# First-layer products with x as two 64-row halves beside each other, pairs two to four

## The chip, the cores and the metric

The kernel runs on one core of a Trainium2 chip. The core has a matrix engine (TensorE, PE in the profile, its weight loads PEld), a vector engine (VectorE, DVE), a scalar engine with function tables (ScalarE, ACT), GpSimd (POOL) and a queue engine that issues most transfers (SyncE, SP). The engines run at the same time, each its own instructions in order, and wait for each other on semaphores. TensorE writes into eight banks of PSUM, each of 128 partitions by 512 numbers of 32 bits; DVE and ACT read them from there. The metric is the time of one execution on the device, in microseconds, as the median of several runs.

## The reference

There are 8 batches of 512 tokens of width 256, and for each batch 64 context rows. The reference computes, per batch:

```python
nx = layer_norm(x, ln_gamma, ln_beta)
q, k, v = nx @ Wq, ctx @ Wk, ctx @ Wv            # v: 64 rows
weights = softmax(q @ k.T / sqrt(256))           # tokens x 64
evidence = weights @ v
combined = concat(nx, evidence, cond)            # width 768
p = softmax(combined @ router_W + router_b)      # 3 experts
h[e] = silu(combined @ e_w1[e] + e_b1[e])        # width 512 for each expert
routed = sum over e of p[e] * (h[e] @ e_w2[e] + e_b2[e])
g = sigmoid(silu(combined @ gate_w1 + gate_b1) @ gate_w2 + gate_b2)
out = x + g * (routed @ out_w + out_b)
```

All of it is in 32-bit floating point. The change touches the part of `h[e]` and of the gate's first layer that comes from `nx` and from `evidence`.

## The kernel before, in words

**Pairs.** The eight batches are worked as four pairs j = 0 to 3. The two batches of a pair, i = 0 and i = 1, share products: a 2 x 2 block of a weight matrix (two halves of the 256 inputs by two chunks of 128 outputs) times a 2 x 2 block of x (two halves of the inputs by two batches) is computed with seven products instead of eight, by sums and differences of the blocks (Winograd's form of Strassen's scheme). The sums over weights are `ws`, those over x are `T` (`combine_x`, L640). `nx_product` (L843) issues one of the seven for a group n of two output chunks: numbers 1, 4, 6 and 7 go into the accumulator `U[n]`, 2 into `Y[n]`, 3 and 5 into `Z[n]`. Group 0 is the gate's first layer (`S["hg"]`), groups 1 to 6 are the experts' 12 chunks, two groups to an expert (`PAIRS`). A product contracts 128 rows: it is one matrix instruction of 128x128 weights by 128x512 data, issued by `product` (L794 to L796).

**Evidence products.** The evidence part needs only 64 rows, since a batch has 64 context rows. The context's values are multiplied with the first layer's weights once per pair (`value_weights`, L771 the products, L778 the copy, L785 a difference), which gives `vw` with batch i in rows 64i to 64i + 63. The softmax weights `wT` lie likewise. `evidence` (L803) issues products of 64 rows, two beside each other: one for batch 0 on rows 0 to 63 and one for batch 1 on rows 64 to 127, into different banks. Each group needs four: into `U`, `Y` and twice into `Z`. In the gate the fourth goes into a bank `W` of its own.

**What is read between the products.** The seven-product form reads an accumulator while it grows. `keep_part` (L838, ACT) copies a state of `U` or `Z` into the chunk of h of one batch, `add` (L835, DVE) adds another accumulator's state to it, `silu` (L829, ACT) applies the function, from h or, for the last, straight from PSUM. `weigh` (L880 and L876, DVE) multiplies h with the router's probabilities `pb` and forms a difference for the second layer.

**Order.** Everything is ordered by hand. For each pair `gate_layer` (L883) comes first and ends with a group of eight evidence products; then `expert_layer` (L927) three times, each ending with eight (the last with four); then `outputs` (L1008), the gate's second layer and the experts' second layers in runs of six or more products. So the first layers hold four groups of evidence products per pair, and full products between them. Steps for the next pair are hung on points of this order by `put` (L1268): `statistics` (L547, L548), `deviation` (L551, ACT, which loads the Sqrt table and afterwards the Silu table), `normalize` (L556, L559), `store_x` (L616, to DRAM on SP's queue), `regroup_x` and `load_x_blocks` (L475, SP's queue), `router_part` (L600), `gate_differences` (L1005), and for the pair itself `router`, `spread_probabilities` (L748 the transposed `prT`; L751 and L755 `pd` and `pb` on POOL's queue) and `value_weights` of expert 2 in expert 1's point "B" (L771). Points of `outputs` are "begin", "gate", "P1", "P5", "P6" and so on.

**Banks.** Each accumulator has a bank by number (`bank`); a new one in the same bank waits until the readers of the former are through. Smaller products take a bank from a list that `spares` sets and `misc` rotates.

Of the kernel before, what the change touches and what calls it, by code (L numbers as in the profile page):

```python
# [8 lines left out]
F32 = mybir.dt.float32  # L9
AF = mybir.ActivationFunctionType  # L10
ALU = mybir.AluOpType
# [5 lines left out]
def kernel(  # L17
# [77 lines left out]

    spare = []

    def bank(i, name):
        return psum.tile([P, 512], F32, tag=f"b{i}", name=name)

    def spares(*banks):
        spare[:] = banks
# [447 lines left out]
    def deviation(j, i):  # L550
        nc.scalar.activation(S["sd", j][:, i, :], S["mv", j][:, i, :, 1], AF.Sqrt, bias=eps_t)  # L551

    def normalize(b):
        mv, sd = (S[n, b // 2][:, b % 2] for n in ("mv", "sd"))
        rstd = work.tile([P, NT], F32, tag="rstd", name=f"rstd_{b}")
        nc.vector.reciprocal(rstd, sd)  # L556
        xn = x_sb[b]
        for t in range(NT):
            nc.vector.tensor_scalar(  # L559
                xn[:, t, :], x_sb[b][:, t, :], mv[:, t, 0:1], rstd[:, t : t + 1], ALU.subtract, ALU.mult  # L560
            )
        S["xn", b] = xn
# [25 lines left out]
            nc.gpsimd.memset(S["lg", j][:, 0, :], 0.0)  # L588
        return S["lg", j]

    def router_part(b):

        j, a = b // 2, b % 2
        lg = logits(j)
        junk = work.tile([P, H], F32, tag="pv", name=f"junk_{b}", bufs=1)
        sums = lg[:, 2, a * NT : (a + 1) * NT]
        if j == 0:
            sums = work.tile([P, NT], F32, tag="ls", name=f"ls_{b}")
        for t in range(NT):
            nc.vector.scalar_tensor_tensor(  # L600
                junk, S["xn", b][:, t, :], 1.0, gg, ALU.mult, ALU.mult, accum_out=sums[:, t : t + 1]
            )
        if j == 0:

            for h in range(2):
                for q in range(NT):
                    nc.gpsimd.tensor_copy(
                        lg[side(a, h), 2, q::NT], sums[q * TB : (q + 1) * TB, 2 * h : 2 * h + 2]
                    )
# [149 lines left out]
    def by_side(flat):  # L759
        return flat.rearrange("p (h t) -> p h t", h=2)  # L760
# [30 lines left out]
    Z_BANKS = ((5, 7), (0, 2), (5, 7))  # L791
    U, Z, Y = {}, {}, {}

    def product(ps, lhsT, rhs, start=False):  # L794

        nc.tensor.matmul(ps, lhsT, rhs, start=start, stop=True, skip_group_check=not start)  # L796

    def fresh(j, e):

# [40 lines left out]
    def hidden(j, q, k, i):  # L840
        return S["h", i, 2 * q // RC][:, (2 * q + k) % RC, :]

    def nx_product(j, n, which, start=False):  # L843
        q = GROUPS[n]
        c = 2 * q
        A, Bx, T_ = S["nxT", 2 * j], S["nxT", 2 * j + 1], S["T", j]

        def a(k, d):
            return w1[:, k, (c + d) * P : (c + d + 1) * P]

        dst, lhsT, rhs = {
            1: (U, a(0, 0), A[:, 0, :]),
            2: (Y, a(1, 0), A[:, 1, :]),
            3: (Z, ws[:, S4, q, :], Bx[:, 1, :]),
            4: (U, a(1, 1), T_[:, 2, :]),
            5: (Z, ws[:, S1, q, :], T_[:, 0, :]),
            6: (U, ws[:, S2, q, :], T_[:, 1, :]),
            7: (U, a(0, 1), Bx[:, 0, :]),
        }[which]
        product(dst[n], lhsT, rhs, start=start)  # L860

    late = []

# [6 lines left out]

    def weigh(j, most):
        for m, i, d in late[:most]:
            q = GROUPS[m]
            if d is None:
                b12 = hidden(j, q, 0, 1)
                nc.vector.tensor_tensor(b12, b12, hidden(j, q, 0, 0), ALU.subtract)  # L876
            else:
                h = hidden(j, q, d, i)
                h = by_side(h)
                nc.vector.tensor_tensor(h, h, S["pb", j][:, i, :, 2 * q // RC, :], ALU.mult)  # L880
        del late[:most]

    def gate_layer(j, steps):  # L883
        n = 0
        for i in range(2):
            for k in range(KH):
                S["hg", i, k] = hpool.tile([P, T], F32, tag=f"hg{i}{k}", name=f"hg_{2 * j + i}_{k}")
        U[n], Z[n], Y[n] = (bank(i, f"ps_{u}_{j}_{n}") for i, u in ((0, "u"), (2, "z"), (3, "y")))
        nx_product(j, n, 1, True)
        keep_part(n, 0, 0, U[n])  # L890
        if j == 0:
            anchor_columns(E)
            anchor_columns(0)
        spares(7, 5)
        nx_product(j, n, 5, True)
        keep_part(n, 1, 1, Z[n])
        nx_product(j, n, 2, True)
        nx_product(j, n, 6)
        keep_part(n, 1, 0, U[n])
        nx_product(j, n, 3)  # L900
        for step in steps.get("gate", ()):
            step()
        nx_product(j, n, 7)
        add(n, 1, 1, U[n])
        for step in steps.get("gate end", ()):
            step()
        W = bank(1, f"ps_w_{j}")
        fresh(j, 0)
        evidence(j, [(m, True) for m in PAIRS[0]], W=W)

        add(n, 0, 0, Y[n])
        add(n, 1, 0, Z[n])
        add(n, 1, 1, W)
        silu(j, n, 0, 0)
# [12 lines left out]
    def expert_layer(j, e, steps):  # L927
# [65 lines left out]
        else:  # L993
            evidence(j, [(m, False) for m in (a, b)])

    gate_sums = {}

    def gate_differences(j):
        (b11, b12), (b21, b22) = [[S["hg", i, k] for i in range(2)] for k in range(2)]
        t2, t3, t4 = (  # L1000
            work.tile([P, T], F32, tag=tag, name=f"g_{name}_{j}", bufs=n)
            for name, tag, n in (("t2", "r21", 1), ("t3", "yb", 2), ("t4", "yb", 2))
        )
        for dst, p, m in ((b12, b12, b11), (t2, b22, b12), (t3, t2, b11), (t4, b21, t2)):
            nc.vector.tensor_tensor(dst, p, m, ALU.subtract)  # L1005
        gate_sums[j] = t2, t3, t4

    def outputs(j, steps):  # L1008
        last = j == NP - 1
# [21 lines left out]
        u, z, y = (bank(i, f"ps_g{n}_{j}") for n, i in (("u", 0), ("z", 2), ("y", 4)))  # L1031
        product(u, gw[0][0], b11, start=True)
        product(z, gw2s[:, S1, :], b12, start=True)
        finish_groups(j, PAIRS[-1])
        nc.scalar.copy(g1, u)
        nc.scalar.copy(g22, z)
        spares(6, 7, 4)
        product(y, gw[0][1], b21, start=True)
        product(u, gw2s[:, S2, :], t2)
        nc.scalar.copy(g2, u)  # L1040
        finish_odd(j, PAIRS[-1])
        gate(0, 0, g1, y)
        product(z, gw2s[:, S4, :], b22)
        gate(0, 1, g2, z)
        product(u, gw[1][0], t3)
        gate(1, 1, g22, u)
        run("begin")
        weigh(j, 99)
        run("gate")

        NQ = NE // 2
# [148 lines left out]
    with tc.manual_schedule(engines=None):  # L1200
# [62 lines left out]
        for j in range(NP):  # L1263
# [38 lines left out]
                put(within, (1, "D"), combine_second, 2)  # L1302
            if j:
                put(within, "gate", value_weights, j, 1, nc.scalar.copy, False)
                put(within, (0, "S"), value_differences, j, 1)
                put(within, (0, "S"), router, j)
                put(within, (0, "S"), spread_probabilities, j)
            if j and j + 1 < NP:
                put(within, (0, "B"), statistics, 2 * j + 3, 0, NT)
            put(within, (0, "C" if j == 0 else "B"), value_weights, j, 2)  # L1310
            put(within, (1, "C"), load_x_blocks, 2 * j)
            put(within, (2, "A"), gate_differences, j)
            put(within, (2, "C"), load_x_blocks, 2 * j + 1)
            if j + 1 < NP:
                b0, b1 = 2 * j + 2, 2 * j + 3
                if j + 2 < NP:
                    put(between, "begin", load_x, b0 + 2)
                    put(between, "begin", load_x, b1 + 2)
                put(within, (0, "A" if j else "D"), statistics, b0, 0, NT)
                if j == 0:  # L1320
                    put(within, (0, "D"), statistics, b1, 0, NT)
                for i in range(2):
                    put(within, (0, "D") if j else (1, "S"), deviation, j + 1, i)
                for b in (b0, b1):
                    put(within, (1, "W" if j else "S"), normalize, b)
                    put(within, (1, "W" if j else "S"), store_x, b)
                put(within, (1, "C"), regroup_x, b0)
                put(within, (1, "A" if j else "B"), router_part, b0)
                put(within, (1, "D" if j else "B"), router_part, b1)
                put(between, "begin", transpose_blocks, b0)  # L1330
                put(between, "gate", regroup_x, b1)
                put(between, "begin", value_weights, j + 1, E)
                put(between, "begin", store_router_rows, j + 1)
                put(between, "begin", spread_router_rows, j + 1)
                put(between, "P5", transpose_blocks, b1)
                put(between, "P2", scores, j + 1)
                put(between, "P2", combine_x, j + 1, nc.gpsimd)
                put(between, "P7", softmax, j + 1)
                put(between, "P7", value_weights, j + 1, 0)
                put(between, "P7", router_logits, j + 1)  # L1340
                put(between, "P3", turn_weights, j + 1)
                put(between, "P3", router_exp, j + 1)
            gate_layer(j, within)
            for e in range(E):
                expert_layer(j, e, within)
            outputs(j, between)


# [32 lines left out]
```

## Time and profile before

| what | value |
|---|---|
| median of 3 runs | 462.18 us (462.06 to 462.39) |
| profiled execution, span | 460.5 us |
| granted clock of TensorE | 1.000 |
| second pair, first product to first product of the third | 142.63 to 248.52 us |
| its first layers, to the first product of the gate's second layer | 142.63 to 201.63 us |
| busy there: TensorE, DVE, ACT | 59.00, 47.70, 33.92 us |

The profiled execution is one run, taken by itself; its span runs from the first instruction to the last, and the runs' time has some microseconds around it (462.18 to 460.5 here, though of different executions). A row of the timeline has the start, the length, the engine, the line of the kernel, the operation, the tile written and the tiles read, shape and count. A product of 32-bit numbers appears as two records of TensorE. TensorE takes the next before the former has ended, so lengths overlap, and the distance from start to start is what a product costs. What stands in brackets after a row is how long the engine was idle before it, and who ended that.

### The profile page before, as it was taken

What the parts mean: (1) busy time and instruction counts of PE and PEld (TensorE: products, weight loads), DVE (VectorE), ACT (ScalarE), POOL (GpSimd) and SP (SyncE); (2) the same over time, 40 slices, a digit from 0 to 9 for tenths busy, and PEclk for the clock granted to TensorE, in tenths of its full rate; (3) what the DMA queues carried; (4) which work ended last, traced back from release to release, by engine and by line L of the source; (5) the groups of instructions that cost most, each with busy time, mean ns of one, the idle gap of its engine ahead of it and who ended that gap; (6) DMA issues with size and microseconds to landing.
All of it is one profiled execution on the core that took longest, in us unless ns stands there. A gap on an engine that the chain in (4) does not pass through costs nothing.

```text
span 460.5 us, 4752 instructions
## 1 busy us (share of the span) xinstructions
PE 456.0 (99%) x1455; PEld 210.2 (46%) x1455; DVE 365.3 (79%) x683; ACT 214.7 (47%) x370; POOL 100.3 (22%) x149
## 2 busy tenths in 40 slices
PE   9999999999999999999999999999999999999997
PEld 7544555444444444444444444444444444444445
DVE  2888979969799669869799659878889625797983
ACT  3445683655222666557221576448231455458000
POOL 6357715002081300001072300001062300000010
PEclk9999999999999999999999999999999999999999
DMA  8974677302013326812011234702011470000004
GB/s 276 370 160 123 104 229 117 95 0 46 7 23 46 73 90 139 156 26 46 6 24 28 41 137 114 114 3 46 6 24 23 74 203 0 0 0 1 0 14 78
DMA packets 119401, 35.27 MB, mean 77 GB/s; under 512 B 106044, under 2 KB 116336, under 8 KB 118864
## 3 DMA queue, kind: packets, MB, share of 16 engines
q1 hardware_dynamic: 115312, 27.02, 28.7%
q0 software_dynamic: 2176, 7.17, 4.8%
q10 hardware_dynamic: 1888, 0.79, 0.6%
q8 instruction: 11, 0.18, 0.2%
q14 instruction: 14, 0.11, 0.1%
HBM read 27.56 MB, written 7.39 MB: 76 GB/s over the span
## 4 chain that ended last, share of the span: by engine, by line
PE 99%; DVE 0%; issue 0%
PE ps_u L796 45%; PE ps_z L796 20%; PE ps_y L796 14%; PE ps_vw L771 5%; PE ps_gu L796 3%; PE ps_w2o L501 2%; PE ps_s L649 2%; PE ps_gz L796 1%; PE ps_tokens L796 1%; PE ps_wake L294 1%; PE ps_v L339 1%; PE ps_m L339 1%; PE ps_gy L796 1%; PE pt_x L579 0%; PE pt_ctx L318 0%; PE ps_ar L440 0%
## 5 line engine op out<-in xcount | busy, mean ns | idle before, releaser
L880 DVE TENSOR_TENSOR h<-h,pb 128x512 f32<-128x512 f32 x96 | 61.9, 693 | 6.5 <-ACT h L829 6.5
L796 PE MATMUL ps_u<-h,w2o 128*128 128x512 f32 x144 | 64.2, 595 | 0.0
L829 ACT ACTIVATE h<-h,abias 128x512 f32<-128x512 f32 x72 | 49.6, 719 | 13.4 <-DVE h L835 12.9
L796 PE MATMUL ps_u<-nxT,w 128*128 128x512 f32 x112 | 55.3, 604 | 0.0
L796 PE MATMUL ps_z<-wT,vw 64*128 64x512 f32 x104 | 49.5, 605 | 0.0
L1105 POOL TENSOR_TENSOR yb<-yb,xb 128x512 f32<-128x512 f32 x14 | 17.8, 1269 | 142.8 <-DVE yb L1104 127.2
L796 PE MATMUL ps_z<-h,w2s 128*128 128x512 f32 x96 | 42.5, 592 | 0.0
L796 PEld LDWEIGHTS ps_u<-h,w2o 128*128 128x128 f32 x144 | 27.0, 190 | 32.7 <-issue 29.4
L838 ACT COPY h<-ps_u 128x512 f32<-128x512 f32 x48 | 28.0, 583 | 29.4 <-PE ps_u L796 29.0
L415 POOL DMA_DIRECT2D vrd<-vw x8 | 5.0, 629 | 137.0 <-ACT vw L778 137.0
L1072 DVE TENSOR_TENSOR h<-h,h 128x1024 f32<-128x1024 f32 x24 | 34.3, 1482 | 0.0
L796 PEld LDWEIGHTS ps_u<-nxT,w 128*128 128x128 f32 x112 | 20.2, 189 | 29.5 <-issue 24.2
L829 ACT ACTIVATE h<-ps_u,abias 128x512 f32<-128x512 f32 x24 | 16.5, 687 | 29.7 <-PE ps_z L796 29.4
L796 PEld LDWEIGHTS ps_z<-h,w2s 128*128 128x128 f32 x96 | 18.2, 190 | 23.0 <-issue 22.3
L796 PE MATMUL ps_y<-nxT,w 128*128 128x512 f32 x56 | 28.6, 592 | 0.0
L796 PE MATMUL ps_z<-T,ws 128*128 128x512 f32 x56 | 28.6, 592 | 0.0
L835 DVE TENSOR_TENSOR h<-h,ps_y 128x512 f32<-128x512 f32 x24 | 16.4, 683 | 15.0 <-PE ps_y L796 14.0
L796 PE MATMUL ps_u<-wT,vw 64*128 64x512 f32 x56 | 27.8, 611 | 0.0
L796 PE MATMUL ps_y<-wT,vw 64*128 64x512 f32 x56 | 27.0, 596 | 0.0
L771 PE MATMUL ps_vw<-w,vT 128*128 128x512 f32 (+1 forms) x64 | 26.9, 542 | 0.0
L796 PE MATMUL ps_u<-T,ws 128*128 128x512 f32 x56 | 26.6, 592 | 0.0
L796 PE MATMUL ps_u<-T,w 128*128 128x512 f32 x56 | 26.6, 592 | 0.0
(229 smaller groups left out, 792.2 us busy)
## 6 DMA issues: line engine op xcount, KB each, us to landing
pb<-pd POOLq DMA_DIRECT2D x4, 1536.0 KB, 6.6
xb<-in_x_dram SPq DMA_DIRECT2D x64, 64.0 KB, 2.5
out_dram<-yb SPq DMA_DIRECT2D x56, 64.0 KB, 2.0
w<-in_L_xcond_e_w_dram SPq DMA_DIRECT2D x6, 512.0 KB, 10.1
x<-in_x_dram SPq DMA_DIRECT2D x24, 128.0 KB, 3.0
xd<-x SPq DMA_DIRECT2D x24, 128.0 KB, 2.4
xg<-xd SPq DMA_DIRECT2D x48, 64.0 KB, 2.4
scr_wa<-in_L_xcond_e_w_dram SPq DMA_DIRECT2D x3, 512.0 KB, 16.8
```

Source lines behind the costliest of these rows:

```text
L339: nc.tensor.matmul(ps, w_sb[:, k, m * P : (m + 1) * P], src[:, k, :], start=(k == 0), stop=(k == KH - 1))
L415: nc.gpsimd.dma_start(S["vrd", j][i].rearrange("e c -> c e"), S["vw", j][row_half(i), R0:])
L501: nc.tensor.matmul(ps[:, d * H : (d + 1) * H], w2T[:, k, (i + d) * P : (i + d + 1) * P], ow_sb[:, k, :], start=(k == 0), stop=(k == KH - 1),)
L649: nc.tensor.matmul(ps[side(i, h), g * NH : (g + 1) * NH], mr[:, k, 2 * j + i, g * TB : (g + 1) * TB], S["nxT", 2 * j + i][:, k, h * NH : ( ...
L771: nc.tensor.matmul(ps, vT[:, k, j * 2 * CT : (j + 1) * 2 * CT], w1[:, KH + k, n0:n1], start=(k == 0), stop=(k == KH - 1),)
L796: nc.tensor.matmul(ps, lhsT, rhs, start=start, stop=True, skip_group_check=not start)
L829: nc.scalar.activation(h, h if src is None else src, AF.Silu, bias=abias[:, c, 2 * j + i : 2 * j + i + 1])
L835: nc.vector.tensor_tensor(h, h, part, ALU.add)
L838: nc.scalar.copy(chunk(n, i, d), part)
L880: nc.vector.tensor_tensor(h, h, S["pb", j][:, i, :, 2 * q // RC, :], ALU.mult)
L1072: nc.vector.tensor_tensor(d, p, m, ALU.subtract)
L1105: nc.gpsimd.tensor_tensor(yb, yb, S["xb", 2 * j + row][:, i, :], ALU.add)
```

## The change

In pairs two to four (j = 1 to 3) the products between the gate's first layer and the last evidence product of expert 3 are issued in another form and another order. `half_layers` takes the place of the three calls of `expert_layer` and of the gate's evidence group. Every product with x of 128 rows becomes two products of 64 rows, one on rows 0 to 63 and one on rows 64 to 127, both accumulating into the same bank. The evidence products stay what they are. `SLOTS` is a list of 57 slots: two half products each, the first on rows 0 to 63, the second on rows 64 to 127, of different accumulators, and after a bar the steps of the other engines. `P1.3` is product 1 with x for group 3 (its first half where it stands first, its second half where it stands second); `U.`, `Y.`, `Z.`, `V.` and `W.` are the evidence products (`V` is the second into `Z`). Of the steps, `k`, `a`, `s` and `w` are `keep_part`, `add`, `silu` and a weighing, `df` the difference, `st`, `nm` and `lg` statistics, normalization and router part of one tile of 128 tokens, `xd`, `xg` and `xb` the transfers, `r` the router and its spreading, `g0` to `g3` the gate's differences. `HOME` gives the bank of each accumulator.

Two halves of one accumulator write the same bank from different rows. `half_product` sees when a bank goes from one half to the other without a reader in between: the former product then counts up a semaphore of the bank, and TensorE waits for it ahead of the next. 43 such waits come in each of the three pairs.

The weighing of the last groups (`LATE`) moves into `outputs` at the points where `finish_groups`, `finish_odd` and `weigh` stood. `value_weights` of expert 2 moves to point "P6" of the pair before, and statistics, normalization and router part are cut into tiles. Pair j = 0 keeps its order, and so do the rest of `outputs` and the gate's products with x, except that product 4 of the gate, formerly in expert 1, is in the list.

```diff
+    def half_product(ps, lhsT, rhs, half, start=False):
+        prior_half, prior = last_half.get(ps.name, (half, None))
+        if prior_half == half or start:
+            ins = product(ps, lhsT, rhs, start)
+        else:
+            tag = bank_of[ps.name]
+            if tag not in finished:
+                finished[tag] = [tc.alloc_semaphore(f"half_{tag}"), 0]
+            finished[tag][1] += 1
+            prior.then_inc(finished[tag][0])
+            group = f"half_{tag}_{finished[tag][1]}"
+            tc.add_to_no_dep_group(group, prior.ins)
+            tc.no_tile_sem_insts.add(prior.ins.name)
+            nc.tensor.wait_ge(*finished[tag])
+            ins = product(ps, lhsT, rhs, start)
+            tc.declare_fence(ins.ins, group=group)
+        last_half[ps.name] = half, ins
...
+    def read_bank(ps):
+        last_half.pop(ps.name, None)
...
 def gate_layer(j, steps):
...
+        if j:
+            return
         W = bank(1, f"ps_w_{j}")
         fresh(j, 0)
...
+    SLOTS = (
+        "Y.0 W.0 | vw",
+        "P2.2 P5.2 | r a00.0",
+        "P1.1 Z.1 | w11.0 s00.0 s11.0",
+        "P4.0 Z.2 | st0.0",
+        "U.0 P1.1 | st0.1 st0.2",
+        "P5.2 Z.0 | k00.1 st0.3",
+        "P1.2 P4.0 | k11.2 a10.0",
+        "P2.3 P5.1 | st1.0 s10.0 st1.1 s01.0",
+        "Y.2 P1.2 | st1.2",
+        "P2.1 V.2 | st1.3 k00.2 g0 dev",
+        "P6.1 P2.2 | g1",
+        "P1.3 P3.2 | a00.2",
+        "P6.2 P6.1 | g2 g3",
+        "P3.2 P1.3 | k10.1 nm0.0",
+        "Y.1 P5.3 | nm0.1 k00.3 nm0.2",
+        "P5.1 Z.3 | nm0.3 xd0 s00.2 nm1.0 nm1.1",
+        "Y.3 P6.2 | k11.1 nm1.2 nm1.3 xd1 xb0 xg xb1",
+        "P7.1 P2.1 | w00.2 k10.2 lg0.0",
+        "P5.3 P2.3 | a10.2",
+        "P6.3 P7.1 | a00.1 s10.2 a00.3 k11.3",
+        "P7.2 V.1 | a11.1 s00.1",
+        "P1.4 P6.3 | w10.2 s00.3 w00.1",
+        "Y.4 P7.2 | s11.1 w00.3 k10.3",
+        "P1.6 P1.4 | a11.2",
+        "U.1 P3.3 | w11.1 s11.2 lg0.1 k00.4",
+        "P4.1 V.3 | w11.2",
+        "U.2 P1.6 | lg0.2 lg0.3",
+        "P4.2 P4.1 | lg1.0 k00.6 lg1.1",
+        "P6.4 P3.1 | s01.1 lg1.2 lg1.3",
+        "P7.3 P4.2 | w01.1",
+        "P3.1 P6.4 | df.2 s01.2",
+        "P6.6 P7.3 | w01.2 k10.4 a10.1",
+        "P3.3 P5.6 | a11.3 s10.1",
+        "P1.5 P6.6 | a10.3 s11.3 w10.1",
+        "P7.4 Z.6 | s10.3 w11.3 k10.6",
+        "P2.4 P1.5 | w10.3",
+        "P4.3 P5.5 | df.1 k00.5 df.3",
+        "U.3 P2.4 |",
+        "P5.6 Z.5 | a00.4",
+        "P6.5 P4.3 | s00.4 k11.6 w00.4",
+        "P7.6 Z.4 | s01.3",
+        "P5.5 P6.5 | w01.3",
+        "P2.5 P7.6 | k10.5 k11.5",
+        "Y.5 P3.6 | a11.6",
+        "Y.6 P7.4 | s11.6 w11.6",
+        "P7.5 P5.4 |",
+        "P4.6 V.5 |",
+        "P5.4 P7.5 |",
+        "U.6 P3.5 | k11.4 a11.5",
+        "P2.6 V.6 | a11.4 s11.5 s11.4 w11.5",
+        "P3.5 P2.5 | w11.4",
+        "P4.5 V.4 | a10.5",
+        "U.5 P2.6 | a00.5 s10.5 s00.5",
+        "U.4 P3.4 | w10.5 a00.6",
+        "P4.4 P4.5 | w00.5 s00.6",
+        "P3.6 P4.6 | df.5 s01.5 w00.6",
+        "P3.4 P4.4 | s01.6 a10.6",
+    )
+    LATE = (
+        "s01.4 a10.4",
+        "s10.6 s10.4",
+        "w01.5 w01.6 w01.4 w10.6 w10.4 df.6 df.4",
+    )
+    HOME = {
+        "U.0": 0, "Z.0": 2, "Y.0": 3, "W.0": 1, "Y.2": 4, "Z.2": 5, "U.1": 6, "Z.1": 7,
+        "U.2": 1, "Y.3": 3, "Y.1": 2, "U.3": 0, "Z.3": 4, "U.4": 5, "Y.4": 2, "U.6": 3,
+        "Z.6": 6, "U.5": 1, "Z.5": 4, "Z.4": 7, "Y.5": 2, "Y.6": 0,
+    }
...
+    def half_layers(j):
...
+        def half(token, k):
+            kind, n = token.split(".")
+            n = int(n)
+            dst, start = target(kind, n)
+            rows = row_half(k)
+            if kind[0] == "P":
+                ps, lhsT, rhs = nx_operands(j, n, int(kind[1]))
+                half_product(ps, lhsT[rows, :], rhs[rows, :], k, start)
+                return
+            c = 2 * GROUPS[n] + (k if kind in ("Y", "Z") and n else 1 - k if n else kind in ("U", "W"))
+            half_product(
+                dst[n], S["vw", j][rows, c * P : (c + 1) * P], S["wT", j][rows, :], k, start
+            )
...
+        for slot in SLOTS:
+            products, steps = slot.split("|")
+            for k, token in enumerate(products.split()):
+                half(token, k)
+            for token in steps.split():
+                step(token)
+        S["late", j] = [lambda t=tokens: [step(x) for x in t.split()] for tokens in LATE]
...
-        finish_groups(j, PAIRS[-1])
+        finish()
...
-        finish_odd(j, PAIRS[-1])
+        finish_silu()
...
-        weigh(j, 99)
+        weigh_last()
...
-            put(within, (0, "C" if j == 0 else "B"), value_weights, j, 2)
...
+                put(between, "P6", value_weights, j + 1, 2)
...
             gate_layer(j, within)
-            for e in range(E):
-                expert_layer(j, e, within)
+            if j:
+                half_layers(j)
+            else:
+                for e in range(E):
+                    expert_layer(j, e, within)
             outputs(j, between)
```

## The prediction

> **What bounds the kernel now.** I read the spans and clocks first (460.5 us, clock 1.000), then the page's busy times and the chain that ended last, then the timeline of TensorE in the second pair, and last ACT and DVE there.
>
> ```profile
> span 460.5 us, 4752 instructions
> ...
> PE 456.0 (99%) x1455; PEld 210.2 (46%) x1455; DVE 365.3 (79%) x683; ACT 214.7 (47%) x370; POOL 100.3 (22%) x149
> ...
> PE 99%; DVE 0%; issue 0%
> ```
>
> TensorE is the chain: DVE, ACT and the queues matter only where they make TensorE wait, and a saving counts only if it is TensorE time. So the question is what TensorE does between two products. The timeline around the third of the four groups of evidence products of this pair (start, length, engine, line, operation, tiles, shape, count):
>
> ```profile
> 182.05 1.88 PE L796 MATMUL ps_u<-T,w 128*128 128x512 f32 x4
> 183.86 0.69 PE L796 MATMUL ps_u<-wT,vw 64*128 64x512 f32 x1
> 183.87 0.69 PE L796 MATMUL ps_z<-wT,vw 64*128 64x512 f32 x1
> 184.40 0.59 PE L796 MATMUL ps_u<-wT,vw 64*128 64x512 f32 x1
> 184.40 0.59 PE L796 MATMUL ps_z<-wT,vw 64*128 64x512 f32 x1
> 184.82 0.59 PE L796 MATMUL ps_u<-wT,vw 64*128 64x512 f32 x1
> ...
> 186.97 0.59 PE L796 MATMUL ps_y<-wT,vw 64*128 64x512 f32 x1
> 186.98 0.59 PE L796 MATMUL ps_z<-wT,vw 64*128 64x512 f32 x1
> 187.50 1.98 PE L796 MATMUL ps_u<-nxT,w 128*128 128x512 f32 x4
> 189.32 1.02 PE L796 MATMUL ps_y<-nxT,w 128*128 128x512 f32 x2
> ```
>
> Every product is two records, and records start 0.429 us apart (twelve in 5.31 us: 11 x 0.429 + 0.592), so a product costs 0.858. Two evidence products already run beside each other, one on rows 0 to 63 and one on rows 64 to 127 (183.86 and 183.87), at the same 0.429. The switch between forms is what costs: from 182.05 to 189.32 stand 4 + 8 + 4 record times, 16 x 0.429 = 6.86, but 7.27 passed. The missing 0.41 is some 0.10 ahead of each first record and 0.10 in it, once going in (183.77 expected, 183.86 seen, then 0.54 to the next), once coming out.
>
> **The change, part by part.** *Removed: three of four groups.* The other groups of this pair lose as much by the same count: 148.64 to 154.19 is 5.55 against 12 x 0.429 = 5.15 (0.40); 166.20 to 173.47 is 7.27 against 6.86 (0.41); 197.90 to 202.59 is 4.69 against 4.29 (0.40). Four groups cost 1.62. The list has one way in (slot 1, at 149.59 as now) and one way out (after slot 57): 0.40 stays, 1.22 goes. Three pairs: 3.66.
>
> *The products themselves: nothing.* The 43 products with x become 86 halves, and 28 evidence products stay: 114 halves in 57 slots of 0.858, 48.9 us. Before it was 43 x 0.858 plus 14 evidence couples x 0.858: the same. No row shows halves that read different tensors beside each other. Below, their price is the evidence couple's 0.429 per record, above, the 0.54 of a couple just after a switch: 57 x 2 x 0.11 = 12.5 us per pair, 37.6 in all. I take 0.429: the couples inside a group go to different banks with different weights and keep it. Issuing is no limit: 32 score products, each with its weight load, pass in 1.93 us, 0.06 each; a slot has four of them.
>
> *value_weights(j, 2)* moves from inside expert 1 to P6 of the pair before: two products, four records, 1.72 of TensorE from one place to another, no difference in the sum. Its copy (0.58 on ACT) and subtraction (0.42 on DVE, L785) now come between these two:
>
> ```profile
> 225.91 0.65 DVE L1088 TENSOR_TENSOR r<-r,ps_u 128x512 f32<-128x512 f32 x1
> 229.50 0.69 DVE L1102 TENSOR_TENSOR r<-r,ps_y 128x512 f32<-128x512 f32 x1 [2.94 <-PE ps_y L796]
> ```
>
> DVE waits 2.94 there, and 1.72 longer with the move, so both are hidden. If that cover went, 1 us a pair would follow.
>
> *Added: 43 waits in each pair* where a bank goes from one half of the rows to the other, on TensorE's own queue, so every later product and weight load is behind each. The shortest distance is two slots (29 of 43). A product's result reaches another engine 1.12 us after its start:
>
> ```profile
> 142.63 1.02 PE L796 MATMUL ps_u<-nxT,w 128*128 128x512 f32 x2
> 143.75 0.59 ACT L838 COPY hg<-ps_u 128x512 f32<-128x512 f32 x1 [1.00 <-PE ps_u L796]
> ```
>
> The second slot starts 1.716 after the first, so the wait ends 0.60 early, 0.41 with a weight load of 0.19 in between, while the slot between them runs. That slot is the cover. I take 0. Below there is no gain in a wait; above, an exposed hand-over costs the 0.10 seen from the end of the second record (143.65) to ACT: 129 x 0.10 = 12.9 us.
>
> The Trainium skill, in TensorE: Matmul & The Clock Gate (Part 3, The cost: per-tile semaphore tail), speaks against this part: it has increments of a semaphore serialize at 26.3 ns each. By the page the 129 new ones would be an estimated 3.4 us, and the sum 461.9. The row disagrees: ACT is released at 185.02 by a product of the group above, so increments happen inside it, and its pitch stays 0.43.
>
> ```profile
> 185.02 0.69 ACT L829 ACTIVATE h<-ps_u,abias 128x512 f32<-128x512 f32 x1 [2.97 <-PE ps_z L796]
> ```
>
> *Steps of DVE and ACT spread over the slots.* Their work in the 49 us, by rows: DVE 39 additions and weighings x 0.61, 8 statistics x 0.53, 8 normalizations x 0.33 with two reciprocals of 0.2, 8 logit parts x 0.47, 4 gate differences x 0.70, 4 further differences x 0.65, 1.3 for the router and vw: 41.5, or 85%. ACT 25 Silu x 0.63, 18 copies x 0.61, two table loads of 1.28 and 0.5 of Sqrt: 29.8, or 61%. There is room; order decides. Slot s starts at 150.55 + (s - 2) x 0.858. The tightest chain I find goes through the two table loads: P1.3 ends in slot 14 (160.85), so its copy k00.3 starts at 161.97, the Silu table load at 162.57, s00.2 at 163.85, w00.2 on DVE at 164.6, lg0.0 at 165.2, a10.2 from 165.7 to 166.4. It frees bank 5 for U.4, which slot 22 opens at 167.71: 1.3 us early. The other reuses of banks that I walked have 1.4 to 2 us. I take 0; from below no gain (TensorE waits nowhere now), above 1.3 us a pair: both table loads (2.57) a second time in that chain, less its reserve.
>
> *Transfers.* POOL issues pd (4) and pb (1) from slot 2: prT is ready at 151.6 instead of 154.5. In the profile pb landed 10.2 after prT (issue at 158.13 and 6.6), which makes 161.8; its first reader is w00.2 at 164.6, 2.8 later. SP keeps its order (xd, xb, xg, xb, 32 issues, 16.4 us), starting about 163.5 instead of 174.7; xg is read at 207.77. Both hidden; a pb later by more than 2.8 lands on the chain above.
>
> **Sum.** 462.18 - 3.66 = 458.5. The profiled execution has a span of 460.5 and lies 1.7 below the median of the runs; the span after should be 456.8.
>
> The same page (Part 3, The mechanism) says that products start strictly in program order. Here the z product, issued second, starts at 183.87, ahead of u's second record at 184.40, so rows of different halves do overtake. By the rule halves would stand 0.43 apart, still 0.858 a slot, with an estimated 0.43 more at each way out: 459.8.
>
> **Rivals.**
> *Waits that show (slower).* Each of the 129 waits empties TensorE's queue, and the next weight load comes late. For it: no wait of TensorE on itself in a dense stretch is in the profile. Against: 0.41 us of reserve. It eats the gain at 3.66 / 129 = 28 ns per wait; at 0.10 the time is 458.5 + 12.9 = 471.4, at 0.05 465.0. It is slower beyond measurement from 36 ns.
> *A step comes late.* DVE at 85%, in order, with pb or the table loads holding it: 0.3 to 1.3 us a pair, 459.4 to 462.4. Against: 1.3 us at the tightest place.
> *The switch isn't saved.* If the 0.1s belonged to the change of operands and not of rows, they would come back wherever evidence and x stand side by side: 462.2 or, with many such slots, more. Against: records go from w with nxT to ws with T and back with nothing between.
>
> **How the numbers follow.** A median can be told from no change at about 0.2%, 0.9 us. Forecast: 0.73 (own range 457.8 to 459.5). Late step: 0.10, a fifth of it at over 0.9 us a pair and so within 0.2%. Waits that show: 0.12, a tenth of it under 21 ns and so still faster, a tenth between 21 and 36. Switch not saved: 0.05, four fifths of it the same time. Faster: 0.73 + 0.08 + 0.01 = 0.82; same: 0.02 + 0.01 + 0.04 = 0.07; slower: 0.10 + 0.01 = 0.11. The range runs from 457.8 (all of 0.41 x 9 and 0.7 for what I can't resolve) to 461.5, a late step of 1 us a pair: 0.73 + 0.08 + 0.01 = 0.82. The far ends, 471 by waits and 496 by couples, stay outside.
>
> **What would show it.** Right: couples of halves 0.429 apart through all 57 slots, evidence and x alike; each pair from second to fourth 1.2 us shorter from slot 1 to the gate's second layer, besides the 1.72 moved; TensorE without idle rows. Wrong: starts 0.5 or more apart after a wait, the two halves of a slot one after the other, or weight loads ending late; then the waits decide. DVE idle behind pb, or TensorE behind an ACT copy at slots 14 to 22, would be the late step.

## The result, and the profile after

The changed kernel takes 458.79 us (median of 4 runs, 458.70 to 459.89) where the kernel before took 462.14 in runs beside it (462.06 to 462.39). The medians lie 3.35 apart. The ratio goes by the means (459.04 and 462.19, since one run of the changed kernel took 459.89): it is 0.9932, with a 95% interval from 0.9918 to 0.9946, which is 3.1 us less, between 2.5 and 3.8. The profiled execution has a span of 456.8 us instead of 460.5, as the sum had it; the rest outside the span is 2.0 us, not 1.7.

The page of the changed kernel, span, busy times and the chain that ended last:

```profile
span 456.8 us, 5304 instructions
...
PE 451.4 (99%) x1713; PEld 211.5 (46%) x1713; DVE 365.1 (80%) x683; ACT 213.9 (47%) x370; POOL 100.2 (22%) x149
...
PE 98%; DMA 1%; DVE 0%; SPq 0%; issue 0%
```

The number of TensorE's records grows from 1455 to 1713: 258 = 3 pairs x 43 products x 2 records, each now a 128-row record cut into two of 64 rows. DVE and ACT have the same work as before, and TensorE is still the chain.

The timeline of TensorE in the changed kernel at the head of the second pair's list, and at its end (start, length, engine, line, operation, tiles, shape, count):

```profile
150.71 0.59 PE L804 MATMUL ps_u<-nxT,w 128*128 128x512 f32 x1
151.23 0.69 PE L804 MATMUL ps_y<-wT,vw 64*128 64x512 f32 x1
151.24 0.69 PE L804 MATMUL ps_w<-wT,vw 64*128 64x512 f32 x1
151.77 0.59 PE L804 MATMUL ps_y<-wT,vw 64*128 64x512 f32 x1
151.77 0.59 PE L804 MATMUL ps_w<-wT,vw 64*128 64x512 f32 x1
152.20 0.59 PE L804 MATMUL ps_y<-nxT,w 64*128 64x512 f32 x1
152.20 0.59 PE L804 MATMUL ps_z<-T,ws 64*128 64x512 f32 x1
152.62 0.59 PE L804 MATMUL ps_y<-nxT,w 64*128 64x512 f32 x1
...
199.84 0.59 PE L804 MATMUL ps_u<-T,w 64*128 64x512 f32 x1
200.36 1.13 PE L804 MATMUL ps_gu<-hg,gw_sb 128*128 128x512 f32 x2
```

The way in is at 151.23, 0.52 after the record before it and 0.54 before the next, and the way out at 200.36. Between them evidence couples and x couples alike start 0.42 to 0.44 apart, in all three lists, and the two halves of a slot start within 0.01 of each other. The three lists last the same. Here is the busy time of the engines of the changed kernel between the first couple and the gate's second layer of each pair (window, its length, then busy time of each engine with its instructions, clock, DMA share, GB/s):

```profile
151.23:200.36 49.13, 49.13 (x230) 22.00 (x229) 41.19 (x95) 30.49 (x48) 3.67 (x7) 1.00 0.49 113
255.93:305.06 49.13, 49.13 (x230) 22.00 (x229) 41.21 (x95) 30.48 (x48) 3.76 (x7) 1.00 0.41 92
360.63:409.75 49.12, 49.12 (x229) 21.99 (x228) 31.72 (x53) 27.57 (x44) 3.65 (x6) 1.00 0.29 60
```

and the same stretch of the second pair in the kernel before:

```profile
149.59:201.63 52.04, 52.04 (x148) 21.93 (x147) 41.47 (x95) 31.31 (x49) 3.67 (x7) 1.00 0.48 107
```

The stretch is shorter by 2.91: 1.72 is expert 2's value product, now ahead of it, and 1.19 are switches. The whole span divides like this (first couples before at 149.59, 255.48 and 361.38):

| stretch | before | after | difference | of it moved value product | rest |
|---|---|---|---|---|---|
| start to first list | 149.59 | 151.23 | +1.64 | +1.72 | -0.08 |
| first list to second | 105.89 | 104.70 | -1.19 | 0 | -1.19 |
| second list to third | 105.90 | 104.70 | -1.20 | 0 | -1.20 |
| third list to end | 99.11 | 96.17 | -2.94 | -1.72 | -1.22 |

The three rests sum to 3.61, nine switches of 0.40. TensorE "busy" was 100% of both windows, 52.04 of 52.04 before: the lost tenths lie in the distances of starts, not in idle rows.

### The profile page after: what moved, and what is told of

The parts are those of the page before. It is cut to its first block, busy times and chain, and to the rows that moved or that the text cites. A ratio compares the mean times of both kernels' runs of the same rounds, so it can differ in the third digit from the quotient of the medians.

```text
span 456.8 us, 5304 instructions
## 1 busy us (share of the span) xinstructions
PE 451.4 (99%) x1713; PEld 211.5 (46%) x1713; DVE 365.1 (80%) x683; ACT 213.9 (47%) x370; POOL 100.2 (22%) x149
## 4 chain that ended last, share of the span: by engine, by line
PE 98%; DMA 1%; DVE 0%; SPq 0%; issue 0%
PE ps_u L804 45%; PE ps_z L804 20%; PE ps_y L804 14%; PE ps_vw L777 5%; PE ps_gu L804 3%; PE ps_w2o L505 2%; PE ps_s L655 2%; PE ps_gz L804 2%; PE ps_tokens L804 1%; DMA scr_ctx<-in_ctx_dram 1%; PE ps_v L343 1%; PE ps_m L343 1%; PE ps_gy L804 1%; PE ps_ar L444 0%; PE ps_kq L356 0%; PE pt_x L585 0%
## 5 line engine op out<-in xcount | busy, mean ns | idle before, releaser
L804 PE MATMUL ps_u<-nxT,w 64*128 64x512 f32 (+1 forms) x184 | 86.9, 592 | 0.0
L919 DVE TENSOR_TENSOR h<-h,pb 128x512 f32<-128x512 f32 x96 | 63.4, 697 | 14.9 <-ACT h L862 12.2
L804 PE MATMUL ps_z<-wT,vw 64*128 64x512 f32 x104 | 51.6, 593 | 0.0
L804 PE MATMUL ps_z<-T,ws 64*128 64x512 f32 (+1 forms) x92 | 46.4, 590 | 0.0
L804 PE MATMUL ps_z<-nxT,ws 64*128 64x512 f32 (+1 forms) x92 | 45.9, 590 | 0.0
L804 PE MATMUL ps_y<-nxT,w 64*128 64x512 f32 (+1 forms) x92 | 45.5, 590 | 0.0
L804 PEld LDWEIGHTS ps_u<-nxT,w 64*128 64x128 f32 (+1 forms) x184 | 33.1, 188 | 26.7 <-issue 24.2
L804 PE MATMUL ps_u<-T,ws 64*128 64x512 f32 (+1 forms) x92 | 42.8, 590 | 0.0
L804 PE MATMUL ps_u<-T,w 64*128 64x512 f32 (+1 forms) x98 | 42.4, 590 | 0.0
L868 DVE TENSOR_TENSOR h<-h,ps_u 128x512 f32<-128x512 f32 x24 | 16.1, 684 | 11.2 <-PE ps_u L804 11.1
```

What stands on the lines that cost most here:

```text
L804: return nc.tensor.matmul(ps, lhsT, rhs, start=start, stop=True, skip_group_check=not start)
L868: nc.vector.tensor_tensor(h, h, part, ALU.add)
```

## The experiments

They ask three things: what a switch costs and whether it is the switch (couples, one_trip, two_trips), what a wait costs (more_waits, near), and how much reserve the tightest chain has (late_one, late_two). The last one (vw_gate) moves the value product. Since the start of the program differed between the profiles by up to 1.4 us (the last section), the length of the list, from first couple to the gate's second layer, is compared, and the times stand beside it.

**couples, one_trip, two_trips.** Three kernels add the same work to each list: two products of 128 rows with a weight tile of zeros, which add nothing to an accumulator. In couples they are four halves, two beside each other after slot 20 and two after slot 40; in one_trip two full products after slot 20; in two_trips one full product at each place.

```diff
+    zt = const.tile([P, P], F32, tag="zt", name="zt")
+    nc.gpsimd.memset(zt, 0.0)
+    def zero_full(n, j):
+        product(U[n], zt, S["nxT", 2 * j][:, 0, :])
+    def zero_couple(j, *ns):
+        for k, n in enumerate(ns):
+            rows = row_half(k)
+            half_product(U[n], zt[rows, :], S["nxT", 2 * j][rows, 0, :], k)
...
-        "P6.3 P7.1 | a00.1 s10.2 a00.3 k11.3",
-        "P6.5 P4.3 | s00.4 k11.6 w00.4",
+        "P6.3 P7.1 | zc31 a00.1 s10.2 a00.3 k11.3",      # couples
+        "P6.5 P4.3 | zc53 s00.4 k11.6 w00.4",
+        "P6.3 P7.1 | zf3 zf3 a00.1 s10.2 a00.3 k11.3",   # one_trip
+        "P6.3 P7.1 | zf3 a00.1 s10.2 a00.3 k11.3",       # two_trips
+        "P6.5 P4.3 | zf5 s00.4 k11.6 w00.4",
```

> The changed kernel with two more couples of 64-row half products in each of pairs two to four, one after slot 20 and one after slot 40. Their weights are zeros, so they add work and nothing to the sums. My theory (a couple costs its two record times and nothing else): 3 x 2 x 0.858 = 5.1 us over the changed kernel, span 456.8 + 5.1 = 461.9. Rival (halves beside each other cost more than a full product, hidden in the balance): more than 6 us.

> The same added work as two full products of 128 rows with zero weights, both after slot 20: the list leaves the 64-row form once and comes back. Theory (the switch of rows is what costs, 0.40 for each way out and back): couples plus 3 x 0.40 = 1.2 us, span 463.1. Rival (the loss is at the change of operands between evidence and x, not of rows): the same as couples, 461.9.

> The same two full products with zero weights, but one after slot 20 and one after slot 40: two ways out and back. Theory: another 3 x 0.40 = 1.2 us over one_trip, span 464.3, and by the same arithmetic three such ways a pair are the 3.7 us which the change gained. Rival (only the added work counts): 461.9 as in the other two.

| kernel | list, us | against the one above | median, us | ratio to before, 95% |
|---|---|---|---|---|
| changed kernel | 49.13 | | 458.79 | 0.9932 [0.9918, 0.9946] |
| couples | 50.84 | +1.71 | 464.49 | 1.0049 [1.0034, 1.0064] |
| one_trip | 51.24 | +0.40 | 465.79 | 1.0079 [1.0064, 1.0094] |
| two_trips | 51.64 | +0.40 | 467.35 | 1.0111 [1.0096, 1.0126] |

The timeline of TensorE in couples, around the zero couples after slot 20:

```profile
168.34 0.59 PE L804 MATMUL ps_u<-nxT,w 64*128 64x512 f32 x1
168.76 1.02 PE L804 MATMUL ps_u<-nxT,zt 64*128 64x512 f32 x4
169.62 0.59 PE L804 MATMUL ps_u<-nxT,w 64*128 64x512 f32 x1
169.62 0.59 PE L804 MATMUL ps_z<-wT,vw 64*128 64x512 f32 x1
170.05 0.59 PE L804 MATMUL ps_u<-nxT,w 64*128 64x512 f32 x1
```

and in one_trip, around the two full products at the same place:

```profile
169.25 0.59 PE L804 MATMUL ps_u<-nxT,w 64*128 64x512 f32 x1
169.77 1.98 PE L804 MATMUL ps_u<-nxT,zt 128*128 128x512 f32 x4
171.68 0.69 PE L804 MATMUL ps_u<-nxT,w 64*128 64x512 f32 x1
...
172.21 0.59 PE L804 MATMUL ps_u<-nxT,w 64*128 64x512 f32 x1
```

In couples four records in two pairs take 168.76 to 169.62, 0.86 = 2 x 0.43, and the next distance is 0.43. In one_trip the full records begin 0.10 late (0.52 after 169.25), and their follower begins 1.91 after them instead of 1.72 (0.10 in the first full record, 0.10 ahead of the couple) with 0.53 to the next: 0.10 ahead and 0.10 in the first record, each way, as the kernel before showed it. The tiles are the same in both (`nxT` and `zt`), so what costs is the number of rows, not another operand. One way out and back costs 0.40, the second in another place another 0.40: the change took out nine, 3.6 us. The spans of the three, 462.2, 464.3 and 465.7, lie 0.3, 1.2 and 1.4 above the expected 461.9, 463.1 and 464.3. All of that lies ahead of the lists: the first evidence couple of pair one comes 0.27, 1.18 and 1.37 later than in the changed kernel (the last section). The rival of a switch that isn't saved has fallen, and with it the thought that more work in the list is slower by itself: 1.71 is the product time.

**more_waits.** Before each half product without a wait, where its bank has a semaphore by then, a wait for the count already reached and waited for is put.

```diff
         if prior_half == half or start:
+            if bank_of[ps.name] in finished:
+                nc.tensor.wait_ge(*finished[bank_of[ps.name]])
             ins = product(ps, lhsT, rhs, start)
```

> The changed kernel with one more wait of TensorE ahead of each half product that had none, on the bank's semaphore at a count that is already reached: over 150 more waits in the three pairs, nothing else. Theory (a wait that is over when the queue gets to it costs nothing): span 456.8 within 0.3. Rival (each wait costs queue time): at the 0.1 us of a hand-over 15 us or more, at 28 ns each over 4 us.

The median is 458.99 (458.75 to 459.16), the ratio to before 0.9930 [0.9914, 0.9947]. The page and the second pair's list (same columns as above):

```profile
span 456.9 us, 5406 instructions
```

```profile
151.36:200.49 49.13, 49.13 (x230) 22.00 (x229) 41.19 (x95) 30.48 (x48) 3.67 (x7) 1.00 0.49 113
```

The edit puts 196 waits (54, 71 and 71 in the three pairs). 102 of them are in the trace as instructions of their own, and 92 more weight loads than in the changed kernel carry a wait. The list is 49.13 as before. A wait that has long been met costs nothing on TensorE's queue; at 28 ns each, the break-even of the prediction's rival, the 102 alone would have been 2.9 us. That leaves waits that are not yet met.

**near.** The products of neighbouring slots are exchanged at 16 places, so that a bank's second half comes in the very next slot for 22 of the 43 waits of a pair. The products are the same, as are the waits; the steps of the other engines stay at their slots.

```diff
-        "P1.1 Z.1 | w11.0 s00.0 s11.0",
-        "P4.0 Z.2 | st0.0",
+        "P4.0 Z.2 | w11.0 s00.0 s11.0",
+        "P1.1 Z.1 | st0.0",
         "U.0 P1.1 | st0.1 st0.2",
-        "P5.2 Z.0 | k00.1 st0.3",
-        "P1.2 P4.0 | k11.2 a10.0",
+        "P1.2 P4.0 | k00.1 st0.3",
+        "P5.2 Z.0 | k11.2 a10.0",
...
```

> The changed kernel with sixteen neighbouring slots of the list exchanged (their products, not the steps of the other engines), so that 22 of the 43 waits per pair, in 19 slots, come in the slot right after the product they wait for. Theory (two slots of distance hide the wait, one does not): a product's result is there 1.12 us after its start, the next slot would start after 0.858 and needs a weight load of 0.19 before: 0.26 to 0.45 lost where both halves of the array are held up, less where only one is: 10 to 26 us, span 467 to 483. Rival (the distance is without effect, the array orders these by itself): 456.8.

One run: 471.58 us, span 469.6, and the list is 53.11, 3.98 longer in each of the pairs. The timeline of TensorE in near, where `U.0 P1.1` follows `P1.1 Z.1`:

```profile
154.75 0.59 PE L804 MATMUL ps_u<-nxT,w 64*128 64x512 f32 x1
...
155.18 0.59 PE L804 MATMUL ps_u<-nxT,w 64*128 64x512 f32 x1
...
155.61 0.59 PE L804 MATMUL ps_u<-wT,vw 64*128 64x512 f32 x1
155.92 0.66 PE L804 MATMUL ps_u<-nxT,w 64*128 64x512 f32 x1
156.04 0.59 PE L804 MATMUL ps_u<-wT,vw 64*128 64x512 f32 x1
```

The first half of P1.1 starts at 154.75 and ends at 155.77. Its second half should stand beside `U.0` at 155.61, but starts at 155.92: the wait is over 1.14 after the start of the product waited for, when its weight load begins:

```profile
155.61 0.19 PEld L804 LDWEIGHTS ps_u<-wT,vw 64*128 64x128 f32 x1 [0.24 <-issue]
155.89 0.34 PEld L804 LDWEIGHTS ps_u<-nxT,w 64*128 64x128 f32 x3
```

Two slots are 1.716, and a weight load starts one record (0.43) ahead of its product, at 1.29: the reserve is 0.15 for the load on its usual place and more for the product. At one slot, 0.858, it is 0.28 late. Not all of the 3.98 comes from such waits. At two other slots the exchange put a product one slot nearer to a step of DVE that it needs, and the weight load waits for DVE:

```profile
159.51 0.18 PEld L804 LDWEIGHTS ps_y<-nxT,w 64*128 64x128 f32 x1 [0.75 <-DVE hg L868]
...
175.41 0.18 PEld L804 LDWEIGHTS ps_u<-wT,vw 64*128 64x128 f32 x1 [0.75 <-DVE h L868]
```

By the starts of the later half, 0.19 and 0.27 are lost there. Some 3.5 remain for the 19 slots that wait for TensorE's own products, 0.19 each. So the rival of waits that show is real at the distance of one slot and absent at two. The near kernel's list in busy times (columns as above) hardly shows the loss as idle time:

```profile
152.07:205.18 53.11, 52.78 (x230) 29.02 (x229) 41.46 (x95) 30.35 (x48) 3.69 (x7) 1.00 0.45 105
```

Of the 3.98, 3.65 stand in TensorE's own busy time (52.78 for 49.13 with the same products). What shows is PEld, 29.02 for 22.00, and the starts.

**late_one, late_two.** In the chain through the two table loads one (late_one) or two (late_two) more table loads, each with a one-column function, are put on ACT before `s00.2`; Silu's load follows them.

```diff
-        "P5.1 Z.3 | nm0.3 xd0 s00.2 nm1.0 nm1.1",
+        "P5.1 Z.3 | nm0.3 xd0 tl s00.2 nm1.0 nm1.1",       # late_one
+        "P5.1 Z.3 | nm0.3 xd0 tl tm s00.2 nm1.0 nm1.1",    # late_two
...
+            "tl": lambda: load_table(AF.Sigmoid),
+            "tm": lambda: load_table(AF.Exp),
```

> The changed kernel with one more table load and a Sigmoid of one column (1.28 + 0.2 = 1.5 us) on ACT just ahead of s00.2, in the chain through the table loads that I called the tightest. Theory (that chain has 1.3 us to spare in pairs two and three; pair four has no Sqrt load and so more): 2 x 0.2 = 0.4 us over the changed kernel, span 457.2. Rival A (no reserve, the list was cut to fit): 1.5 for each of two or three pairs, 459.8 to 461.3. Rival B (the chain isn't the tightest and has far more to spare): 456.8.

> The same with two more table loads, 3.0 us. Theory: 2 x (3.0 - 1.3) = 3.4 us, span 460.2. Rival A (no reserve): 462.8 to 465.8. Rival B (far more reserve): 456.8 to 457.

One run each: 460.49 and 465.63 us, spans 458.1 and 463.6; the lists are 49.45 and 50.95, and they are so in all three pairs (0.32 and 1.82 longer). That pair four, with fewer table loads, would be less delayed was expected and is wrong: the Sqrt load lies ahead of `k00.3`, which waits for a product anyway, and so the chain behind `k00.3` is the same with or without it. ACT in the changed kernel (pair two):

```profile
163.57 0.59 ACT L871 COPY h<-ps_u 128x512 f32<-128x512 f32 x1 [0.25 <-PE ps_u L804]
164.17 1.28 ACT L862 ACT_TABLE_LOAD   x1
165.47 0.72 ACT L862 ACTIVATE h<-h,abias 128x512 f32<-128x512 f32 x1
...
166.56 0.59 ACT L871 COPY h<-ps_u 128x512 f32<-128x512 f32 x1
```

and the first record of slot 21 there:

```profile
168.51 0.59 PE L804 MATMUL ps_z<-wT,vw 64*128 64x512 f32 x1
```

In late_one the same copy, and the same record of TensorE with the next one of its slot:

```profile
168.48 0.59 ACT L871 COPY h<-ps_u 128x512 f32<-128x512 f32 x1
169.12 0.69 PE L804 MATMUL ps_z<-wT,vw 64*128 64x512 f32 x1
169.66 0.59 PE L804 MATMUL ps_z<-wT,vw 64*128 64x512 f32 x1
```

In late_two ACT:

```profile
168.55 1.28 ACT L862 ACT_TABLE_LOAD   x1
...
170.94 0.59 ACT L871 COPY h<-ps_u 128x512 f32<-128x512 f32 x1
```

and TensorE in late_two, slots 20 and 21:

```profile
169.43 0.59 PE L804 MATMUL ps_u<-nxT,w 64*128 64x512 f32 x1
171.58 0.69 PE L804 MATMUL ps_u<-nxT,w 64*128 64x512 f32 x1 [1.56 <-ACT h L871]
...
172.11 0.59 PE L804 MATMUL ps_u<-nxT,w 64*128 64x512 f32 x1
```

The last copy is `k10.2`, of `U.2`, which `P7.2` in slot 21 adds to; it ends at 171.53, and slot 21 starts 0.05 later. In the changed kernel it ends at 167.15, and slot 21 starts at 168.51: 1.36, less the 0.05, is a reserve of 1.30. Both sizes come out of that. Late_one delays the copy by 1.52 against its list: 1.52 - 1.30 = 0.22, and a start after a stop costs another 0.10 (0.53 to the next record), 0.32. Late_two delays it by 3.02: 1.72 and 0.10, 1.82. So a delay in this chain is free up to a reserve of 1.3 us; beyond that it costs what exceeds the reserve, and the 0.10. Both spans lie above the theory's 457.2 and 460.2: a third pair is delayed, each stop costs the 0.10, and the program starts 0.3 and 1.4 later. That puts late_two's 463.6 inside the range of rival A, but the lists speak against A: without a reserve they would have grown by 1.52 and 3.02, not by 0.32 and 1.82.

**vw_gate.** The value product of expert 2 goes from P6 of the pair before to the gate's layer of its own pair, still ahead of the list.

```diff
                 put(within, "gate", value_weights, j, 1, nc.scalar.copy, False)
+                put(within, "gate", value_weights, j, 2)
...
-                put(between, "P6", value_weights, j + 1, 2)
```

> The two products of value_weights for expert 2 stand in the gate's layer of their own pair again (pairs two to four), no longer at P6 of the pair before; the list and everything in it is as in the changed kernel. Theory (a product moved among full-row products costs 1.72 us wherever it stands, its copy and its difference are hidden): the list keeps its 49.13 us from first couple to the gate's second layer, the distance from one list's first couple to the next stays 104.70, the first list begins 1.72 earlier than in the changed kernel (149.5) and the last part after the third list is 1.72 longer; time 458.8 within 0.4. Rival (the place at P6 is what was worth something, because value_weights used to hold TensorE between expert 1 and 2): the distance from list to list grows, by up to 1.2 us, and the time goes to 460 to 462. Second rival (the place at P6 itself costs, by the copy and difference between the output additions): the time falls below 458.4.

The median is 459.17 (458.91 to 459.65), the ratio to before 0.9931 [0.9915, 0.9948]; the lists are 49.13, 49.12 and 49.12, the distances from list to list 104.70, and the part from the third list to the end 96.17, all as in the changed kernel. The expected shifts of the first list and the last part were wrongly worked out: the gate's layer lies ahead of the list, so the product is ahead of it in both kernels. What differs is the start of the program, 0.56 later at the first evidence couple (31.89 for 31.33). So the place of this product is worth nothing either way, and both rivals have fallen for these two places. Its former place, between experts 1 and 2, wasn't tried again.

## Why the prediction was right, point by point

*The switch, 0.40 each and nine of them (3.66).* Right: 1.19, 1.20 and 1.22 by the table of stretches, 3.61; one_trip and two_trips give 0.40 for one such way by itself. That the span is met to the tenth (456.8) is in part luck: the start of the program differs by 1.4 from profile to profile, and by 0.1 in these two.

*The products: nothing, 0.429 a record.* Right, at the lower bound. Halves that read different tensors, the row that was missing before, start together at 0.42 to 0.44 (152.20 and 152.20 with `w` and `ws`). The upper bound of 0.54 belongs to the switch, and to a start after a stop.

*The waits: nothing.* Right at two slots, by 129 waits in the changed kernel and 196 further ones in more_waits. The reserve was put at 0.60 and 0.41 with a weight load. By near the hand-over takes 1.14 to the load, not 1.12 to the product, and a load's usual place is 1.29 after the start: 0.15 there. The sign held, and the cover named (the slot between) is what near takes away. The upper end, 0.10 for an exposed wait, was too low: it was 0.31 in the row shown and 0.19 over 19 slots.

*The value product moved.* Right in sum: +1.72 ahead of the first list, -1.72 after the third. But the list was dated from 149.59 "as now", though the moved product stands ahead of it; it begins at 151.23, and all times that the prediction gives for the chain and the transfers are 1.64 early. As both ends of each comparison move alike, no reserve changed by it.

*The steps of DVE and ACT.* Right: 41.5 and 29.8 of busy time were counted, 41.19 and 30.49 measured in the second pair's list.

*The chain through the table loads, reserve 1.3.* The size came out right with the wrong last link, which is luck. Walked on 1.64, the prediction has `w00.2` at 166.2 and `a10.2` to 168.0; it was 166.22 and 167.87, 1.5 before slot 22. The tightest reader is the copy `k10.2`, which slot 21 waits for: 1.30 by both late runs. It stands on ACT behind `s00.2`, and the prediction's chain, which goes over to DVE there, passed it over.

*Transfers: `pb` 2.8 early.* Nearly right in pair three, too much in pairs two and four, without effect on TensorE. POOL in the changed kernel, pair two and then pair three:

```profile
153.69 2.00 POOL L757 DMA_DIRECT2D pd<-prT  x4 [1.47 <-DVE prT L754]
158.55 0.56 POOL L761 DMA_DIRECT2D pb<-pd  x1 [2.85 <-DMA pd<-prT]
...
262.13 0.55 POOL L761 DMA_DIRECT2D pb<-pd  x1 [1.64 <-DMA pd<-prT]
```

and in near, pair two:

```profile
157.86 0.56 POOL L761 DMA_DIRECT2D pb<-pd  x1 [1.31 <-DMA pd<-prT]
```

In pair two `prT` was ready at 153.39 (the predicted 151.6, 1.64 on, is 153.24). The wait for `pd` was 2.85 where the kernel before had 1.32: `pd` took 3.1 to land instead of 1.6. `pb` landed 6.4 after 158.55, at 165.0, and its first reader is at 166.22: 1.3 are left, not 2.8. In pair three the wait was 1.64, as in the kernel before, and 2.4 are left.

What differs in pair two is a packet of 16 KB on a DMA queue that the page lists as "instruction": it begins at 155.19 and takes 1.45. Fifteen of the sixteen parts of each of the four `pd` transfers had landed by 156.73, the last part of each landed between 157.67 and 158.13. In pairs two and three of all ten profiles, `pb` is issued 4.3 to 5.2 after the first `pd` in the nine cases where such a packet begins in between, and 3.3 to 3.7 in the eleven where none does. That the late parts went through the same DMA engine as the packet is likely and not shown. The transfers of the last pair's output are not the reason: in near they are issued at the same distance before `pd`, and the wait is 1.31. The prediction carried one landing time over from one pair, and the packet is not in it.

In pair four `pb` itself came last. It landed 7.4 after its issue at 367.55, and DVE waited for it:

```profile
375.00 0.69 DVE L919 TENSOR_TENSOR h<-h,pb 128x512 f32<-128x512 f32 x1 [2.63 <-DMA pb<-pd]
```

That is one of the signs of a late step that the prediction named. It cost TensorE nothing: DVE has no work for a next pair there and was early, so that this weighing still starts 0.62 ahead of its place in the lists of pairs two and three, and the list is 49.12.

*The two rules of the Trainium skill, TensorE: Matmul & The Clock Gate, Part 3.* By The cost: per-tile semaphore tail 26.3 ns for each of 129 increments gave an estimated 461.9. The time is 458.79, and the increments show nowhere, in distances or in list length. That section gives its figure for the tail behind a group of packed products; in this dense stream the next products run on beside the increments. By The mechanism the strict order gave 459.8, since the prediction read the rule as one on records. The halves of a slot don't stand 0.43 apart, so this reading has fallen. The products themselves do start in the order of their issue (183.86 and 183.87 in the kernel before, 151.23 and 151.24 here), so the trace doesn't contradict what the section says of whole products, as the prediction took it to.

*The median, 458.5.* It is 0.29 off because the part outside the span is 2.0 us in this kernel (458.79 - 456.80, and 2.0 in most of the experiments) against 1.7 before. The prediction carried the 1.7 over unchanged. What the 0.3 is, no trace shows, and it wasn't tried.

## What to carry to other kernels

Where TensorE is the bound and its busy share says 99%, read the distances between starts: the 0.1 lost at each change from full to half rows stands in no idle column. Work that can be cut to the form of its neighbours, here to 64 rows, saves the switch if each wait it brings looks back far enough for the result to be seen in time: here a result is seen 1.14 us after its product's start, so two slots of 0.858 were enough and one was not. Measure the reserve of the tightest chain by delaying it twice by known amounts: both must give the same reserve, as they did here (1.30).

## What the runs showed that was not expected

The start of the program differs from profile to profile. The first evidence couple of pair one, before anything that the experiments differ in but the small zero tile, came at 31.33 (changed kernel), 31.43 (before), 31.46 (more_waits), 31.60 (couples), 31.62 (late_one), 31.89 (vw_gate), 32.18 (near), 32.51 (one_trip), 32.69 (late_two) and 32.70 us (two_trips). That is 1.4 us of span, more than one pair's share of the change (1.2). In two_trips the product that it hangs on waits for a transfer from DRAM:

```profile
8.40 1.52 PE L343 MATMUL ps_v<-scr_ctx,scr_w 128*128 128x512 f32 x3 [1.15 <-DMA scr_w<-in_L_xcond_Wv_dram]
```

In the changed kernel it starts without such a wait:

```profile
7.21 1.96 PE L343 MATMUL ps_v<-scr_ctx,scr_w 128*128 128x512 f32 x4
```

One run of the changed kernel itself has a span of 457.9 beside 456.7 to 456.8 of the other three. Whether the kernel's edit or chance sets the start wasn't settled, with one profile of each. For differences below 1 us, list lengths from one profile say more than spans.

TensorE that has stopped pays 0.10 when it starts again, without any change of rows: after the stops of late_one and late_two the next distance is 0.53. And two halves that have come out of step run on beside each other: in near the halves after the stop start at 156.85 and 156.90, 0.05 apart, and need no common start to keep the pace.
